# Values projected when they are made: a per-tile product by the value matrix moved into the preparation of the values (layer 0 of a two-layer attention kernel)

## Chip, cores and metric

The kernel runs on one core of one Trainium2 chip. The metric is the device time of one launch in microseconds (us). TensorE is called PE (its weight loads PEld), VectorE DVE, ScalarE ACT, GpSimd POOL and SyncE SP, as in the profile.

## The reference

Input x has 4 batches of 128 channels and 64 x 64 = 4096 tokens. Layer 0 is full attention on group-normalised x with 64-wide queries and keys and 128-wide values; layer 1 is causal attention on layer-normalised tokens, followed by a recurrent network. All data are fp32.

```python
# layer 0; xf = group norm of x, as (b, c, n)
q = einsum('oc,bcn->bon', Wq, xf) + bq
k = einsum('oc,bcn->bon', Wk, xf) + bk
v = einsum('oc,bcn->bon', Wv, xf) + bv
probs = softmax(einsum('bci,bcj->bij', q, k), axis=-1)
x = x + einsum('bcj,bij->bci', v, probs)
# layer 1; t = x as tokens (b, n, c)
t = t + causal_attention(ln(t), Wq1, Wk1, Wv1)
t = t + ffn(ln(t), W, V, gamma, beta)     # batch norm, then y = sigmoid(Wx_t + V y) over the tokens
```

The weights of each value's sum add up to one, so the projection by Wv can be done before or after that sum, and the bias bv is simply added to x.

## The kernel before

X is held with channels on the 128 partitions and tokens along the free axis. Queries are worked on in tiles of 512 tokens (8 tiles a batch), keys in units of 256 tokens. The batches run one after the other, and in each the 8 tiles of layer 0 and then the 8 tiles of layer 1. A layer-0 tile has 16 units; layer 1 is causal, so its tile c has 2(c+1) units. The work of one unit is:

- `score`: products of keys and queries into the PSUM pair `ps` (four fp32r products on L895 in layer 0, four records for two fp32 products on L888 in layer 1), and ACT's exp into the SBUF tile `s` (L897, L901; three `s` buffers);
- `product`: DVE adds `s` to the running `total` (L929; L924 for the first unit), and PE multiplies the values by `s` into the PSUM accumulator `av` (L932, two fp32 products, which the profile shows as four records).

The score of a unit is written ahead of the product of the unit before it. The values of layer 0, `V0`, are kept in the buffer that is later WX of the last batch, so the profile calls them `WX` in the rows of L932; those of layer 1 are called `V`.

The small work between the units is written as generators which a hand-made list (`todo`, and `ends` for the endings of tiles) steps once a unit. The final order on each engine is then set by a scheduler with priorities, which keeps this order nearly everywhere. The generators that matter here:

- `keys0(b, c)` prepares 512 keys and values of layer 0. DVE makes the normalised `xn` (called `xg`, L644; two buffers), POOL adds the bias B0v to X in place (L646), PE makes `pk` = keys and queries (L649), ACT and DVE split the keys into high and low parts (L652 to L661; QR, L654, holds the later queries), PE transposes `xn` in four blocks of 128 tokens (L665), and ACT copies the result into `V0` (L666). The eight calls of batch 0 stand at the start and under its first tile; those of batch b+1 stand within layer 1 of batch b.
- `finish` ends a tile. DVE adds the two halves of `total` (`t`, L765), sums over partitions by two 32x32 transposes, small copies and reductions (L767 to L780), and forms `o` = av / sum, scaled by GUARD (L782). Two steps later PE multiplies `o` by the value matrix into `po` (L788: W0v or W1v), and DVE adds `po` / GUARD to X (L794).
- `prepare1` then makes layer 1's values from the new X: PE transposes (L688), DVE takes statistics (L692 to L694) and normalises (L721), POOL takes the root (L561).
- `query1` makes layer 1's queries: `pq` on PE (L730), `q` on DVE (L732). `ffn` prepares the recurrence input (L741 to L757).

`pk`, `pt`, `po`, `pq` and the like share two PSUM buffers, handed out by `misc`. The recurrence (L1000 to L1021) follows after all batches, and a flag at the end decides whether a general kernel runs again.

Of the kernel before, what the change touches and what calls it, by code (L numbers as in the profile page):

```python
# [23 lines left out]
ALU = mybir.AluOpType  # L27
# [3 lines left out]
P = 128  # L31
QT = 512
# [430 lines left out]
GUARD = 2.0**40  # L463
# [11 lines left out]
def fast_kernel(  # L475
# [9 lines left out]
    nc = tc.nc  # L485
# [14 lines left out]
    X, X2 = {}, {}  # L500
# [14 lines left out]
    def load(src, shape, name):  # L515
        t = const.tile(shape, F32, name=name)
        nc.scalar.dma_start(out=t, in_=src)
        return t
# [8 lines left out]
    W0v = load(w0v, [P, C], "W0v")  # L527
    W1v = load(w1v, [P, C], "W1v")
# [6 lines left out]
    ident = const.tile([P, P], F32, name="ident")  # L535
# [27 lines left out]
    with ExitStack() as actx:  # L563
# [10 lines left out]
        def misc(name):  # L574
            return ps_m.tile([P, QT], F32, tag="m", name=name)

        gn, K0, QR, V0, V1, Q, R1, wt = {}, {}, {}, {}, {}, {}, {}, {}
# [57 lines left out]
        def keys0(b, c):  # L635

            if c == 0:
                K0[b] = kv.tile([P, N], F32R, tag="K0", name=f"K0_{b}")
                QR[b] = kv.tile([P, N // 2], F32, tag="QR", name=f"QR_{b}")
                V0[b] = WX[B - 1].rearrange("p l s -> p (l s)").rearrange("p (n c) -> p n c", c=C)  # L640
            xn = tmp.tile([P, QT], F32, tag="x", name=f"xg_{b}_{c}", bufs=2)
            gmv, grs = gn[b]
            xt = X[b][:, ts(c, QT)]
            nc.vector.tensor_scalar(xn, xt, gmv[:, 0:1], grs, ALU.subtract, ALU.mult)  # L644

            nc.gpsimd.tensor_scalar(xt, xt, B0v, None, ALU.add)  # L646
            yield
            pk = misc(f"pk_{b}_{c}")
            nc.tensor.matmul(pk, lhsT=W0qk.rearrange("p h o -> p (h o)"), rhs=xn, start=True, stop=True)  # L649
            k = tmp.tile([P, QT], F32, tag="k", name=f"k_{b}_{c}")  # L650
            low, up = slice(0, CQ), slice(CQ, P)
            nc.scalar.activation(k[up, :], pk[up, :], AF.Identity, bias=B0qk[up, :])  # L652
            half, col = divmod(c, NQ // 2)
            nc.vector.tensor_scalar(  # L654
                QR[b][ds(half * CQ, CQ), ts(col, QT)], pk[low, :], B0qk[low, :], None, ALU.add
            )
            yield
            high = tmp.tile([P, QT], F32, tag="h", name=f"kh_{b}_{c}", bufs=2)
            nc.vector.tensor_scalar(high[up, :].bitcast(I32), k[up, :].bitcast(I32), HIGH, None, ALU.bitwise_and)
            nc.vector.tensor_tensor(K0[b][up, ts(c, QT)], k[up, :], high[up, :], ALU.subtract)  # L660
            nc.scalar.copy(K0[b][low, ts(c, QT)], high[up, :])  # L661
            yield
            pt = misc(f"pt0_{b}_{c}")
            for j in range(4):
                nc.tensor.transpose(pt[:, ts(j, P)], xn[:, ts(j, P)], ident)  # L665
            nc.scalar.copy(V0[b][:, 4 * c : 4 * c + 4, :], pt.rearrange("p (j c) -> p j c", j=4))  # L666
            yield

        def query0(b, c):
# [90 lines left out]
        def finish(b, layer, c, off, w, av, total):  # L760

            name = f"{layer}_{b}_{c}_{off}"
            k = w // 32
            t = tmp.tile([P, QT], F32, tag="a", name=f"t_{name}")[:, :w]
            nc.vector.tensor_tensor(t, total[:, 0, :w], total[:, 1, :w], ALU.add)  # L765
            tt = tmp.tile([P, QT], F32, tag="b", name=f"tt_{name}")[:, :w]
            nc.vector.transpose(tt, t)  # L767
            part = small.tile([P, 16], F32, tag="part", name=f"part_{name}")
            nc.vector.tensor_reduce(part[:, :k], tt.rearrange("p (k j) -> p k j", j=32), AX.X, ALU.add)
            yield  # L770
            side = small.tile([32, 4, 16], F32, tag="side", name=f"side_{name}")
            for q in range(4):
                nc.vector.tensor_copy(side[:, q, :k], part[ds(32 * q, 32), :k])
            z = small.tile([P, 16], F32, tag="z", name=f"z_{name}")
            nc.vector.tensor_reduce(z[0:32, :k], side[:, :, :k].rearrange("j q k -> j k q"), AX.X, ALU.add)
            nc.vector.reciprocal(z[0:32, :k], z[0:32, :k])
            for q in range(1, 4):
                nc.vector.tensor_copy(z[ds(32 * q, 32), :k], z[0:32, :k])
            rb = tmp.tile([P, 16, 32], F32, tag="a", name=f"rb_{name}")[:, :k, :]
            nc.vector.transpose(rb, z[:, :k].unsqueeze(2).to_broadcast([P, k, 32]))  # L780
            o = tmp.tile([P, QT], F32, tag="b", name=f"o_{name}")[:, :w]
            nc.vector.scalar_tensor_tensor(  # L782
                o, rb.rearrange("p k j -> p (k j)"), GUARD, av[:, :w], ALU.mult, ALU.mult
            )
            yield
            yield
            po = misc(f"po_{name}")[:, :w]
            nc.tensor.matmul(po, lhsT=W1v if layer else W0v, rhs=o, start=True, stop=True)  # L788
            cols = ds(c * QT + off, w)
            xt = X[b][:, cols]  # L790
            if layer and c == 0:
                X2[b] = xpool.tile([P, N], F32, tag="X2", name=f"X2_{b}")
            dst = X2[b][:, cols] if layer else xt
            nc.vector.scalar_tensor_tensor(dst, po, 1.0 / GUARD, xt, ALU.mult, ALU.add)  # L794
            yield


# [35 lines left out]
        def begin_tile(b, layer, c):  # L833

            if layer == 0:
                if c == 0 and b:
                    for k in range(NQ):
                        whole(("k0", b, k))
                    put(("q0", b, 0), query0(b, 0))
                if c == 1 and b == 0:  # L840
                    put(("m1",), merge1())
                if c == 3 and 0 < b < B - 1:
                    for k in range(NQ):
                        whole(("f", b - 1, k, 0))
                    load_x(b + 1)
                if c == (5 if b else 2) and b + 1 < B:
                    put(("gn", b + 1), gn_stats(b + 1))
                if c == NQ - 1:
                    put(("q1", b, 0), after(b, 0))
                whole(("q0", b, c))  # L850
                if c + 1 < NQ:
                    put(("q0", b, c + 1), query0(b, c + 1))
            else:
                if c == 0 and b + 1 < B:
                    whole(("gn", b + 1))
                    for k in range(NQ):
                        put(("k0", b + 1, k), keys0(b + 1, k))
                whole(("q1", b, c))
                if (b, 1, c) in following:
                    d = following[b, 1, c]  # L860
                    todo.insert(0, ("q1", b, d))
                    made["q1", b, d] = after(b, d)
# [47 lines left out]
        def product(i):  # L910
# [30 lines left out]
            if u == n - 1:  # L941
                for key in list(ends):
                    whole(key)
                key = ("e", b, layer, c, off, w)
                made[key] = finish(b, layer, c, off, w, av, total)
                ends.append(key)
# [9 lines left out]
        for k in range(NQ):  # L956
            put(("k0", 0, k), keys0(0, k))
# [12 lines left out]
    with ExitStack() as fctx:  # L970
# [75 lines left out]
        for b in range(B):  # L1046
            for h in range(2):
                cols = ts(h, N // 2)
# [71 lines left out]
```

## Time and profile before

| what | value |
|---|---|
| median of 3 runs | 2593.09 us (2592.93 to 2595.2) |
| the profiled execution | 2594.39 us, its span 2592.4 us |
| mean granted TensorE clock | 0.991 |
| DVE / ACT / POOL busy | 68% / 44% / 8% |
| HBM read / written | 15.14 MB / 14.68 MB |

A row of the profile names line, engine, operation and "out<-in" by the program's tile names without buffer numbers, then the number of records. An fp32 product appears as two matmul records and two weight loads, a transpose as one of each: so L788's 32 products by W0v show as x64, and the 32 x 4 transposes of L665 as x128. The ends of matmul records are modelled, and rows of one engine may overlap. "Idle" after a bar is time in which the engine stood still just before such a row, with what ended it.

### The profile page before, as it was taken

What the parts mean: (1) busy time and instruction counts of PE and PEld (TensorE: products, weight loads), DVE (VectorE), ACT (ScalarE), POOL (GpSimd) and SP (SyncE); (2) the same over time, 40 slices, a digit from 0 to 9 for tenths busy, and PEclk for the clock granted to TensorE, in tenths of its full rate; (3) what the DMA queues carried; (4) which work ended last, traced back from release to release, by engine and by line L of the source; (5) the groups of instructions that cost most, each with busy time, mean ns of one, the idle gap of its engine ahead of it and who ended that gap; (6) DMA issues with size and microseconds to landing.
All of it is one profiled execution on the core that took longest, in us unless ns stands there. A gap on an engine that the chain in (4) does not pass through costs nothing.

```text
span 2592.4 us, 21739 instructions
## 1 busy us (share of the span) xinstructions
PE 2519.8 (97%) x7372; PEld 1345.1 (52%) x7372; DVE 1760.3 (68%) x3513; ACT 1139.7 (44%) x1386; POOL 219.7 (8%) x297
## 2 busy tenths in 40 slices
PE   7999999999999999999999999999999999999975
PEld 4555554444555555444555555444455555544552
DVE  7776667567867667666876666765786766776564
ACT  4444444444444444444444444444444444344444
POOL 2010001101000100010100010110100000000005
PEclk9999999999999999999999999999999999999988
DMA  2000000000100000000100000000010000000013
GB/s 72 1 0 1 0 1 13 9 4 4 37 0 1 0 1 5 13 5 8 37 0 1 1 0 1 13 9 5 5 37 0 1 1 1 0 1 1 0 65 131
DMA packets 11943, 31.28 MB, mean 12 GB/s; under 512 B 2096, under 2 KB 2864, under 8 KB 10032
## 3 DMA queue, kind: packets, MB, share of 16 engines
q1 hardware_dynamic: 8928, 24.12, 2.6%
q10 hardware_dynamic: 2896, 5.71, 0.6%
q8 instruction: 59, 0.97, 0.2%
q14 instruction: 60, 0.49, 0.1%
HBM read 15.14 MB, written 14.68 MB: 12 GB/s over the span
## 4 chain that ended last, share of the span: by engine, by line
PE 89%; DVE 6%; issue 2%; ACT 1%; POOL 1%; DMA 0%; SPq 0%; POOLq 0%; ACTq 0%; DVEq 0%
PE av L932 48%; PE ps L895 17%; PE ps L888 17%; PE po L788 2%; DVE total L929 1%; PE py L1020 1%; PE pq L730 1%; PE pk L649 1%; POOL rstd_f L561 1%; PE pw_f L747 1%; ACT WX L1021 1%; PE pt L688 1%; DVE lst_f L692 0%; PE pt L665 0%; DVE w_f L751 0%
## 5 line engine op out<-in xcount | busy, mean ns | idle before, releaser
L929 DVE TENSOR_TENSOR total<-total,s 128x1024 f32<-128x1024 f32 (+4 forms) x802 | 881.6, 1103 | 553.4 <-ACT s L897 308.9
L932 PE MATMUL av<-s,WX 128*128 128x512 f32 x2048 | 964.4, 593 | 3.4 <-ACT s L897 3.4
L897 ACT ACTIVATE s<-ps,shift 128x1024 f32<-128x1024 f32 x512 | 569.2, 1114 | 772.9 <-PE ps L895 749.0
L895 PE MATMUL ps<-q,K 128*128 128x512 f32 x2048 | 759.7, 493 | 2.1 <-DVE K L660 1.5
L901 ACT ACTIVATE s<-ps,zero,R 128x512 f32<-128x512 f32 (+1 forms) x590 | 399.9, 729 | 458.9 <-PE ps L888 458.3
L932 PEld LDWEIGHTS av<-s,WX 128*128 128x128 f32 x2048 | 382.2, 189 | 312.0 <-issue 270.0
L895 PEld LDWEIGHTS ps<-q,K 128*128 128x128 f32 x2048 | 386.7, 189 | 291.0 <-issue 236.3
L932 PE MATMUL av<-s,V 128*128 128x512 f32 (+3 forms) x1180 | 504.7, 549 | 0.6 <-ACT s L901 0.6
L888 PE MATMUL ps<-q,X 128*128 128x512 f32 (+3 forms) x1180 | 501.9, 548 | 0.0
L888 PEld LDWEIGHTS ps<-q,X 128*128 128x128 f32 x1180 | 222.6, 190 | 239.7 <-issue 228.2
L932 PEld LDWEIGHTS av<-s,V 128*128 128x128 f32 x1180 | 218.8, 191 | 226.1 <-issue 201.6
L561 POOL TENSOR_TENSOR rstd<-rstd,mhalf 128x4 f32<-128x4 f32 x32 | 32.7, 1022 | 1015.5 <-DVE rstd L560 1015.5
L904 POOL TENSOR_SCALAR_AFFINE_SELECT s<-s 128x128 f32<-128x128 f32 x128 | 46.5, 367 | 523.0 <-ACT s L901 522.4
L646 POOL TENSOR_SCALAR X<-X,B0v 128x512 f32<-128x512 f32 x32 | 59.6, 1865 | 243.8 <-DVE xg L644 238.1
L794 DVE SCALAR_TENSOR_TENSOR X<-po,X 128x512 f32<-128x512 f32 (+1 forms) x65 | 44.1, 678 | 51.3 <-PE po L788 50.9
L752 ACT COPY WX<-w_f 128x512 f32<-128x512 f32 (+1 forms) x33 | 35.3, 1069 | 93.1 <-DVE w_f L751 93.1
L561 POOL TENSOR_TENSOR rstd_f<-rstd_f,mhalf 128x4 f32<-128x4 f32 (+1 forms) x33 | 36.1, 1094 | 398.6 <-DVE rstd_f L560 398.6
L721 DVE TENSOR_SCALAR V<-pt,lmv,rstd 128x128 f32<-128x128 f32 x128 | 43.7, 404 | 35.8 <-POOL rstd L561 35.8
L788 PE MATMUL po<-o,W1v 128*128 128x512 f32 (+1 forms) x66 | 34.4, 604 | 16.1 <-DVE o L782 16.1
L679 DVE TENSOR_TENSOR q<-QR,qh 64x512 fp32r<-64x512 f32 x64 | 43.9, 685 | 6.3 <-PE ps L895 5.7
L765 DVE TENSOR_TENSOR t<-total 128x512 f32<-128x512 f32 (+1 forms) x65 | 44.5, 684 | 4.5 <-PE pfw L605 2.5
L782 DVE SCALAR_TENSOR_TENSOR o<-rb,av 128x512 f32<-128x512 f32 (+1 forms) x65 | 43.9, 675 | 4.4 <-DVE rb L780 0.5
(124 smaller groups left out, 1312.5 us busy)
## 6 DMA issues: line engine op xcount, KB each, us to landing
X<-in_x SPq DMA_DIRECT2D x28, 256.0 KB, 5.5
kept<-X SPq DMA_DIRECT2D x24, 256.0 KB, 2.0
Y<-kept SPq DMA_DIRECT2D x6, 1024.0 KB, 7.6
out<-Y SPq DMA_DIRECT2D x3, 1024.0 KB, 9.7
out<-Y ACTq DMA_DIRECT2D x3, 1024.0 KB, 10.2
X<-in_x ACTq DMA_DIRECT2D x4, 256.0 KB, 5.6
out<-X SPq DMA_DIRECT2D x1, 1024.0 KB, 16.1
out<-X ACTq DMA_DIRECT2D x1, 1024.0 KB, 12.6
```

The source lines that it names most:

```text
L561: nc.gpsimd.tensor_tensor(dst, dst, mhalf[:, :n], ALU.pow)
L646: nc.gpsimd.tensor_scalar(xt, xt, B0v, None, ALU.add)
L765: nc.vector.tensor_tensor(t, total[:, 0, :w], total[:, 1, :w], ALU.add)
L788: nc.tensor.matmul(po, lhsT=W1v if layer else W0v, rhs=o, start=True, stop=True)
L794: nc.vector.scalar_tensor_tensor(dst, po, 1.0 / GUARD, xt, ALU.mult, ALU.add)
L888: nc.tensor.matmul(ps[:, h, first[h] : w], lhsT=lhsT, rhs=q[:, off + first[h] : off + w], start=True, stop=True,)
L895: nc.tensor.matmul(ps[:, h, :], lhsT=lhsT, rhs=q[:, k, :], start=k == 0, stop=k == 1)
L897: nc.scalar.activation(s, ps, AF.Exp, bias=shift)
L901: nc.scalar.activation(part, ps[:, h, first[h] : w], AF.Exp, scale=scale, bias=zero)
L904: nc.gpsimd.affine_select(out=edge, in_=edge, pattern=[[1, P]], base=0, channel_multiplier=-1, compare_op=ALU.is_ge, fill=0.0,)
L929: nc.vector.tensor_tensor(t, t, s[:, h, f:w], ALU.add)
L932: nc.tensor.matmul(av[:, first[h] : w], lhsT=V[:, 2 * u + h, :], rhs=s[:, h, first[h] : w], start=u == 0 and h == 0, stop=u == n - 1 and h ...
```

## The change

In `keys0` the four transposes become four products with the same blocks of `xn` as the stationary operand and W0v as the moving one: `V0` then holds the projected values with tokens on the partitions. In `finish`, layer 0 no longer multiplies `o` by W0v: DVE adds `o` / GUARD to X directly in the step that made `o`, and the generator ends two steps earlier. Layer 1's ending is as it was.

```diff
         def keys0(b, c):
...
-            pt = misc(f"pt0_{b}_{c}")
+            pv = misc(f"pv_{b}_{c}")
             for j in range(4):
-                nc.tensor.transpose(pt[:, ts(j, P)], xn[:, ts(j, P)], ident)
-            nc.scalar.copy(V0[b][:, 4 * c : 4 * c + 4, :], pt.rearrange("p (j c) -> p j c", j=4))
+                nc.tensor.matmul(pv[:, ts(j, P)], lhsT=xn[:, ts(j, P)], rhs=W0v, start=True, stop=True)
+            nc.scalar.copy(V0[b][:, 4 * c : 4 * c + 4, :], pv.rearrange("p (j c) -> p j c", j=4))
...
         def finish(b, layer, c, off, w, av, total):
...
-            yield
-            yield
-            po = misc(f"po_{name}")[:, :w]
-            nc.tensor.matmul(po, lhsT=W1v if layer else W0v, rhs=o, start=True, stop=True)
             cols = ds(c * QT + off, w)
             xt = X[b][:, cols]
-            if layer and c == 0:
+            if layer == 0:
+                nc.vector.scalar_tensor_tensor(xt, o, 1.0 / GUARD, xt, ALU.mult, ALU.add)
+                yield
+                return
+            yield
+            yield
+            po = misc(f"po_{name}")[:, :w]
+            nc.tensor.matmul(po, lhsT=W1v, rhs=o, start=True, stop=True)
+            if c == 0:
                 X2[b] = xpool.tile([P, N], F32, tag="X2", name=f"X2_{b}")
-            dst = X2[b][:, cols] if layer else xt
-            nc.vector.scalar_tensor_tensor(dst, po, 1.0 / GUARD, xt, ALU.mult, ALU.add)
+            nc.vector.scalar_tensor_tensor(X2[b][:, cols], po, 1.0 / GUARD, xt, ALU.mult, ALU.add)
             yield
```

In the changed program one line is added above these, so its line numbers are one higher up to the start of `finish` and four higher from its end on (the products by W1v stand on L795, the new addition on L789).

More of the change, by code (lines that the diff above doesn't have):

```diff
@@ L784, in finish @@
             )
+            cols = ds(c * QT + off, w)
+            xt = X[b][:, cols]
+            if layer == 0:
+                nc.vector.scalar_tensor_tensor(xt, o, 1.0 / GUARD, xt, ALU.mult, ALU.add)
+                yield
+                return
             yield
@@ L787, in finish @@
             po = misc(f"po_{name}")[:, :w]
-            nc.tensor.matmul(po, lhsT=W1v if layer else W0v, rhs=o, start=True, stop=True)
-            cols = ds(c * QT + off, w)
-            xt = X[b][:, cols]
-            if layer and c == 0:
+            nc.tensor.matmul(po, lhsT=W1v, rhs=o, start=True, stop=True)
+            if c == 0:
                 X2[b] = xpool.tile([P, N], F32, tag="X2", name=f"X2_{b}")
-            dst = X2[b][:, cols] if layer else xt
-            nc.vector.scalar_tensor_tensor(dst, po, 1.0 / GUARD, xt, ALU.mult, ALU.add)
+            nc.vector.scalar_tensor_tensor(X2[b][:, cols], po, 1.0 / GUARD, xt, ALU.mult, ALU.add)
             yield
```

## The prediction

> **What bounds the kernel now.** I read the page from the top (busy shares, the span in slices, the chain by engine), then the groups of instructions by form, then two stretches of the timeline, then one window sum. From the page:
>
> ```profile
> span 2592.4 us, 21739 instructions
> ...
> PE 2519.8 (97%) x7372; PEld 1345.1 (52%) x7372; DVE 1760.3 (68%) x3513; ACT 1139.7 (44%) x1386; POOL 219.7 (8%) x297
> ...
> PE   7999999999999999999999999999999999999975
> ...
> PE 89%; DVE 6%; issue 2%; ACT 1%; POOL 1%; DMA 0%; SPq 0%; POOLq 0%; ACTq 0%; DVEq 0%
> ```
>
> TensorE (PE) is nine or ten tenths busy in every slice but the first and the last two, and it holds 89% of the chain that ended last. A busy row alone doesn't prove a bound, so I look at the spacing of its instructions. The timeline of PE, columns start, length, what, count:
>
> ```profile
> 78.18 0.38 PE L601 MATMUL pm<-wm 128*128 128x128 f32 x2
> 78.40 1.88 PE L932 MATMUL av<-s,WX 128*128 128x512 f32 x4
> ...
> 148.36 0.60 PE L688 MATMUL pt<-ident,X 128*128 128x128 f32 x4
> 148.80 1.88 PE L932 MATMUL av<-s,WX 128*128 128x512 f32 x4
> ...
> 175.26 1.02 PE L788 MATMUL po<-o,W0v 128*128 128x512 f32 x2
> 176.12 1.88 PE L932 MATMUL av<-s,WX 128*128 128x512 f32 x4
> ```
>
> The lengths overlap; the starts tell what an instruction costs the queue. One fp32 product of 128x512 is two records and moves the next start by 0.86 us (175.26 to 176.12). Four transposes of 128x128 are four records and move it by 0.44 us (148.36 to 148.80), 0.11 each. One fp32 product of 128x128 is two records and moves it by 0.22 us (78.18 to 78.40). These are the three prices of this change. How often the old ones occur, from the groups by form (mean and idle behind the bar):
>
> ```profile
> L788 PE MATMUL po<-o,W0v 128*128 128x512 f32 x64 | 32.7, 593 | 0.8 <-DVE o L782 0.8
> L665 PE MATMUL pt<-ident,xg 128*128 128x128 f32 x128 | 20.3, 282 | 0.0
> ```
>
> The last column matters most: before all 32 products by W0v together PE idled 0.8 us, before the 128 transposes not at all. They stand in a full queue, so what is taken out or put in moves the end, except where PE would have waited anyway.
>
> **What the Trainium skill says.** Perfetto Trace Analysis, section Tensor Engine Instruction: the profiler estimates a matmul's end, it does not observe it. The trace agrees: the rows above say 593 ns for a record whose successor starts 430 ns later; so I use starts. TensorE: Matmul & The Clock Gate, Part 4, gives about 275 ns for a transpose in a kernel; the mean here, 282 ns, agrees as a length, but the spacing of 110 ns decides for throughput. The same page, section LDWEIGHTS, gives columns/1.2 in ns: an estimate of 107 ns for the 128 columns of one weight load. The trace's load rows are longer (146 ns for the transposes, 188 for po by W0v) but are lengths too; the 0.22 us for two records with two loads says that 110 ns suffice. This prices the worst case below. Part 1 of that page says that an idle PE gets half its clock; the trace has that at a stall of 2.1 us before 655.37, after which the four av records at 657.77 last 3.00 us instead of 1.88.
>
> **The change part by part.** There are 4 batches x 8 tiles = 32 layer-0 tiles, each 16 units.
>
> 1. The product at each tile's end goes: 32 x 0.86 = -27.5 us of PE.
> 2. Four transposes become four fp32 products with xn as stationary operand: 4 x (0.22 - 0.11) = 0.44 us more a tile, 32 x 0.44 = +14.1 us. Eight of these tiles are prepared at the start, 24 during layer 1, at the same places of PE's order. Layer 1 of the trace shows PE full there, so nothing hides them. Bounds for a record: 0.107 (the skill's load) to 0.19 us (a whole load row exposed), see the third rival. I take 0.11 since the 128x128 row shows it. The first two tiles run at half clock (their four transposes end 1.06 us after they start, against 0.60 later), so theirs is 0.88 each; the first is on the starting chain, the second lies in the 0.65 us that PE now waits before 21.14 for q, which is as late as the first. Together again 0.9, no correction. W0v's load is issued at 9.00 and lands in 2.0 us, long before 15.8; the DMA queues of SP and ACT keep their order.
> 3. ACT's copy into V0 is the same 128x512 copy (583 ns), 0.44 us later; ACT is 44% busy and waits for PE before most of its exps. DVE's xg of the tile after next reuses the buffer that these products read, so it starts 0.44 us later; in layer 1 DVE prepares it a tile ahead. Nothing.
> 4. X's addition reads o in SBUF instead of po in PSUM: the trace has no such form of it, the nearest rows are this one from PSUM (687 ns) and t from SBUF twice (692 ns). Nothing. It moves directly behind o on DVE, ahead of one to three total additions, where it waited for po before. Seen at 171 us on DVE:
>
> ```profile
> 171.78 0.69 DVE L782 SCALAR_TENSOR_TENSOR o<-rb,av 128x512 f32<-128x512 f32 x1
> 172.39 1.22 DVE L929 TENSOR_TENSOR total<-total,s 128x1024 f32<-128x1024 f32 x1
> 173.96 1.23 DVE L929 TENSOR_TENSOR total<-total,s 128x1024 f32<-128x1024 f32 x1 [0.35 <-ACT s L897]
> 176.32 0.69 DVE L794 SCALAR_TENSOR_TENSOR X<-po,X 128x512 f32<-128x512 f32 x1 [1.14 <-PE po L788]
> ```
>
> DVE's 1.14 us of waiting goes, and it is worth nothing by itself. The two totals behind start up to 0.6 us later; ACT's exp waits for them only through the three s buffers, three units of 2.65 us away.
>
> 5. The next step, layer 1's transposes of X (L688), now stands on PE three units after the tile's end, where po stood, no longer five. Its wait is for X instead of o. Here o ends at 172.47 and po starts at 175.26: 2.8 us of slack, of which the addition takes 0.6. For the tiles up to the seventh of each batch that slack is 1.9 to 3.5 us, apart from the very first tile (0.06 us, and 0.80 us of PE idle). So no new wait, except at the first tile, where X comes 0.6 us after o and the transposes a little later than po: I credit 0.3 us of the 0.8 (bounds 0 and 0.8).
>
> 6. At the start PE waits three times for K on DVE (0.29, 1.00 and 0.20 us idle before 41.98, 49.78 and 70.35). The products put in ahead of these waits may fall into them: credit 0.6 us, bounds 0 and 1.3.
>
> 7. What is late next: the passage from layer 0 to layer 1, where layer 1's tiles are two and four units long and each brings its own ending and query to DVE.
>
> ```profile
> 383.60:405.50 21.90, 21.90 (x61) 10.74 (x59) 21.00 (x62) 8.09 (x13) 3.02 (x8) 1.00 0.00 0
> ```
>
> ```profile
> 404.71 0.74 DVE L654 TENSOR_SCALAR QR<-pk,B0qk 64x512 f32<-64x512 f32 x1
> ...
> 405.51 1.12 PE L730 MATMUL pq<-X,M 128*128 128x512 f32 x2
> ```
>
> The first is a window sum (length, then PE, PEld, DVE, ACT, POOL busy), the second the timeline: DVE is 21.0 of 21.9 us busy, which with the gaps between 62 instructions is full. The pq at 405.51 starts just when DVE has read pk (404.71 + 0.74 = 405.45), whose PSUM buffer it needs; PE waits 0.25 us there already. This stretch loses the po of the eighth tile on PE but nothing on DVE, so PE arrives 0.86 us sooner and waits 0.86 us longer. The three batches with a next batch have this pk: +2.6 us given back, bounds 0 and 2.6. The fourth has no pk and keeps its gain.
>
> Sum: -27.5 + 14.1 - 0.3 - 0.6 + 2.6 = -11.7 us. The profiled execution took 2594.39 us (2592.4 of span and 2.0 around it), 1.3 above the median of 2593.09. So 2582.7 beside the profiled one, and **2581.4 us** as a median.
>
> **Rivals.**
> - The boundary costs nothing, DVE catching up because it no longer idles for po earlier: 2593.1 - 14.3 = 2578.8. For: 1.1 us of DVE idle vanishes at most tiles. Against: DVE starts the dense stretch at the same PE event, with no backlog to save.
> - The tile ends keep PE waiting: DVE takes X late in its order and the transposes find it missing, as at the first tile. It needs over 1.3 us more delay than I see; if it happened by 0.2 us at 28 tiles, +5.6: 2587. Slack measured on o speaks against it.
> - **Slower:** eight weight loads in a row are not hidden under products of only 128 columns. Place: each pv group. A record then costs the whole load, 0.19 us: 8 x 0.19 = 1.52 a tile instead of 0.88, 32 x 0.64 = +20.5, total +8.8: 2601.9. It decides from about 0.155 us a record, where 256 records eat the 11.7. For: such loads come only in twos or threes now, with wider products between. Against: the 0.22 us of L601, and four transposes with a load each at 0.11.
> - The change doesn't do what it says: V0 is read by av alone and both endings write X in place, so one W0v product replaces the other; nothing speaks for it.
>
> **How the numbers follow.** Forecast 0.70, no cost at the boundary 0.15, waits at tile ends 0.09, exposed loads 0.06. The half-clock spell after a stall, 1.7 us, occurs at one of three layer-1 ends now and may come or go with the phase: it and the bounds of steps 5 to 7 widen both sides. Range 2577.0 to 2587.5. A measurement here can tell about 0.2%, 5.2 us, from no change: 2587.9 is the border. Faster 0.90, same 0.04, slower 0.06.
>
> **What would show it.** Right: the L688 rows of layer 0 at po's places without PE idle; pv rows spaced 0.88 us a tile; pq at the boundary with some 1.1 us of waiting for QR; no DVE row X waiting for po in layer 0. Wrong: pv at 1.2 us or more a tile, or idle before L688 at most tiles.

## The result, and the profile after

The changed kernel takes 2579.97 us (median of 5 runs, 2578.95 to 2581.84), against 2593.09 us before (5 runs, 2591.53 to 2596.02): a ratio of 0.9947, 95% interval 0.9936 to 0.9958, or 13.1 us less. The forecast was 2581.4. The profiled execution took 2581.84 us with a span of 2580.0; before, 2594.39 and 2592.4. Between the two profiled executions lie 12.55 us, and 12.4 of span.

The page of the changed kernel, in the parts that were read before:

```profile
span 2580.0 us, 21857 instructions
...
PE 2510.6 (97%) x7436; PEld 1350.5 (52%) x7436; DVE 1761.0 (68%) x3513; ACT 1140.3 (44%) x1386; POOL 227.7 (9%) x297
...
PE   7999999999999999999999999999999999999975
...
PE 88%; DVE 8%; issue 2%; POOL 1%; ACT 1%; POOLq 0%; DVEq 0%; ACTq 0%
```

PE has 64 records more and is busy 9.2 us less; the slices are the same. The count is easily read wrongly: 64 wide records went (0.43 us each by their spacing), 128 transposes went and 256 narrow records came (0.11 each). DVE's share of the chain has grown from 6% to 8%.

The groups by form, with the idle time before them in the last column:

```profile
L666 PE MATMUL pv<-W0v,xg 128*128 128x128 f32 x256 | 35.4, 284 | 0.0
L789 DVE SCALAR_TENSOR_TENSOR X<-o,X 128x512 f32<-128x512 f32 x32 | 22.1, 691 | 0.9
L689 PE MATMUL pt<-ident,X 128*128 128x128 f32 x128 | 19.2, 272 | 0.7 <-DVE X L789 0.7
L731 PE MATMUL pq<-X,M 128*128 128x512 f32 x64 | 33.0, 597 | 2.9 <-DVE QR L655 2.9
```

The new products find no idle PE, so they are paid in full where PE is full. The addition to X lasts 691 ns with `o` in SBUF and 687 with `po` in PSUM. The transposes behind it wait once, for 0.7 us, at the first tile; the other 31 groups find X ready. And `pq` now waits 2.9 us for DVE's read of `pk`, in three places. The timeline has the four places that the forecast named (columns: start, length, engine, line, what, count, and idle before it):

```profile
94.60 0.68 DVE L789 SCALAR_TENSOR_TENSOR X<-o,X 128x512 f32<-128x512 f32 x1
...
95.34 0.66 PE L689 MATMUL pt<-ident,X 128*128 128x128 f32 x4 [0.75 <-DVE X L789]
...
172.50 0.69 DVE L789 SCALAR_TENSOR_TENSOR X<-o,X 128x512 f32<-128x512 f32 x1
...
175.25 0.60 PE L689 MATMUL pt<-ident,X 128*128 128x128 f32 x4
175.68 1.88 PE L936 MATMUL av<-s,WX 128*128 128x512 f32 x4
...
399.37 1.02 PE L795 MATMUL po<-o,W1v 128*128 128x512 f32 x2
...
400.58 0.74 DVE L655 TENSOR_SCALAR QR<-pk,B0qk 64x512 f32<-64x512 f32 x1
...
401.37 1.13 PE L731 MATMUL pq<-X,M 128*128 128x512 f32 x2 [0.97 <-DVE QR L655]
...
481.04 1.05 PE L666 MATMUL pv<-W0v,xg 128*128 128x128 f32 x8
481.93 1.88 PE L936 MATMUL av<-s,V 128*128 128x512 f32 x4
```

At 175.25 the transposes stand where `po` stood at 175.26, and X is ready since 173.19 (172.50 + 0.69), 2.06 us earlier. At 481.04 eight records of the new products move the next start by 0.89 us. At the passage from layer 0 to layer 1, `pq` could start 0.86 us after `po` and starts 2.00 us after it, when DVE has read `pk` (400.58 + 0.74 = 401.32): a loss of 1.14 us, where it was 0.15 before (`po` at 404.50, `pq` at 405.51).

How the gain builds up is best seen at the tiles' ends, the start of DVE's first ending row (`t`, L765 before, L766 after) in both traces:

| end of | before | after | difference |
|---|---|---|---|
| batch 0, layer 0, first tile | 81.34 | 83.19 | +1.85 |
| batch 0, layer 0, eighth tile | 383.67 | 379.41 | -4.27 |
| batch 0, layer 1, eighth tile | 644.50 | 643.44 | -1.06 |
| batch 1, layer 0, eighth tile | 1000.74 | 993.74 | -7.00 |
| batch 1, layer 1, eighth tile | 1261.55 | 1257.78 | -3.77 |
| batch 3, layer 0, eighth tile | 2233.26 | 2222.78 | -10.48 |
| batch 3, layer 1, last whole tile | 2469.32 | 2457.98 | -11.34 |

Layer 0 gains about 0.85 us a tile (batch 1: 7.00 - 1.06 = 5.94 over seven tiles); layer 1, where the next batch's values are made, gives back 3.2 us a batch. Batch 3 prepares nothing and gives nothing back.

### The profile page after: what moved, and what is told of

It reads as the page before. It is cut to its first block, busy times and chain, and to the rows that moved or that the text cites. A ratio compares the mean times of both kernels' runs of the same rounds, so it can differ in the third digit from the quotient of the medians.

```text
span 2580.0 us, 21857 instructions
## 1 busy us (share of the span) xinstructions
PE 2510.6 (97%) x7436; PEld 1350.5 (52%) x7436; DVE 1761.0 (68%) x3513; ACT 1140.3 (44%) x1386; POOL 227.7 (9%) x297
## 4 chain that ended last, share of the span: by engine, by line
PE 88%; DVE 8%; issue 2%; POOL 1%; ACT 1%; POOLq 0%; DVEq 0%; ACTq 0%
PE av L936 47%; PE ps L899 17%; PE ps L892 16%; PE py L1024 2%; DVE total L933 2%; PE po L795 1%; PE pv L666 1%; PE pk L650 1%; PE pq L731 1%; PE pw_f L748 1%; POOL rstd_f L562 1%; PE pt L689 1%; DVE lst_f L693 0%; DVE t L766 0%; ACT s L901 0%
## 5 line engine op out<-in xcount | busy, mean ns | idle before, releaser
L908 POOL TENSOR_SCALAR_AFFINE_SELECT s<-s 128x128 f32<-128x128 f32 x128 | 46.4, 367 | 536.1 <-ACT s L905 535.6
L647 POOL TENSOR_SCALAR X<-X,B0v 128x512 f32<-128x512 f32 x32 | 67.6, 2115 | 251.1 <-DVE xg L645 249.6
L795 PE MATMUL po<-o,W1v 128*128 128x512 f32 (+1 forms) x66 | 34.8, 609 | 16.1 <-DVE o L783 16.1
L766 DVE TENSOR_TENSOR t<-total 128x512 f32<-128x512 f32 (+1 forms) x65 | 44.4, 683 | 4.4 <-PE pfw L606 2.5
L662 ACT CAST K<-kh 64x512 fp32r<-64x512 f32 x32 | 19.7, 617 | 62.3 <-DVE kh L660 62.3
L768 DVE STREAM_TRANSPOSE tt<-t 128x512 f32<-128x512 f32 (+1 forms) x65 | 45.6, 702 | 1.9
```

The costliest lines, as they stand in the source:

```text
L795: nc.tensor.matmul(po, lhsT=W1v, rhs=o, start=True, stop=True)
L908: nc.gpsimd.affine_select(out=edge, in_=edge, pattern=[[1, P]], base=0, channel_multiplier=-1, compare_op=ALU.is_ge, fill=0.0,)
```

## The experiments

The theory: PE's queue sets the time, and the change is the difference of two prices on it, less a wait at the passage. The rivals: one of the prices is other than its row says (hidden work, exposed weight loads); or DVE's earlier addition is what helps. Each kernel was run 5 to 10 times beside runs of the kernel before, whose median was 2593.51 us beside e1 to e4, 2594.73 beside e5 and e6 (on another chip than the others) and 2593.88 beside e7 to e9. The distances to the changed kernel given below are differences of medians from different sessions, so about 1 us in them means little; the ratios are each to the session's own kernel before.

| kernel | median us (range) | ratio to before, 95% interval |
|---|---|---|
| e1, no projection | 2569.83 (2568.86 to 2572.11) | 0.9910, 0.9896 to 0.9923 |
| e2, both projections | 2604.64 (2602.18 to 2604.71) | 1.0038, 1.0025 to 1.0052 |
| e3, products twice | 2606.01 (2605.81 to 2608.42) | 1.0047, 1.0033 to 1.0061 |
| e4, QR on ACT | 2575.76 (2573.91 to 2576.94) | 0.9927, 0.9914 to 0.9941 |
| e5, po later | 2584.94 (2581.82 to 2586.69) | 0.9964, 0.9950 to 0.9977 |
| e6, e4 and e5 | 2580.91 (2578.79 to 2582.62) | 0.9947, 0.9934 to 0.9961 |
| e7, other work held | 2587.90 (2585.81 to 2590.68) | 0.9977, 0.9968 to 0.9986 |
| e8, e4 and e7 | 2586.04 (2582.63 to 2588.46) | 0.9969, 0.9958 to 0.9979 |
| e9, X added later | 2579.91 (2579.48 to 2581.89) | 0.9945, 0.9932 to 0.9959 |

### The two halves apart: e1 and e2

e1 changes the changed kernel, and leaves the projection by W0v out:

```diff
-                nc.tensor.matmul(pv[:, ts(j, P)], lhsT=xn[:, ts(j, P)], rhs=W0v, start=True, stop=True)
+                nc.tensor.transpose(pv[:, ts(j, P)], xn[:, ts(j, P)], ident)
```

> The changed kernel with the four transposes put back in keys0, so that layer 0's values are never projected: only the removal half of the change. If PE's queue sets the time, this takes off the 27.5 us of the 32 products by W0v, gives back about 3 us of longer waiting at the three passages to layer 1, and costs nothing at the values: some 26 us below the kernel before, about 2567. Rival (the removal was partly hidden, and the new products cost less than 0.22 us each): 20 us or less below. Rival (loads exposed, the new products cost about 1 us a tile more than transposes): over 40 us below.

e2 changes the kernel before, and projects layer 0's values twice:

```diff
-                nc.tensor.transpose(pt[:, ts(j, P)], xn[:, ts(j, P)], ident)
+                nc.tensor.matmul(pt[:, ts(j, P)], lhsT=xn[:, ts(j, P)], rhs=W0v, start=True, stop=True)
```

> The kernel before with the four transposes replaced by the four products by W0v, and the product at the tile's end kept, so that layer 0's values are projected twice: only the added half. PE's queue theory: 24 tiles prepared in layer 1 cost 0.45 us each, 10.8, and the eight at the start 1.5 to 3.6 us since PE waits there: 12 to 14.5 us above before, 2605 to 2607.5. The wait of pq for QR stays at 0.25 us, since nothing was taken from the passage. If the loads were exposed: 32 x 1.08 = 34 us above. With e1 the two halves should add up to the change (-13.1).

Measured: the removal alone -23.7 us, the addition alone +11.1 (against their session's 2593.51). Together -12.6, where the change gave -13.1: the halves add up within what the runs scatter. Each is smaller than expected. For the removal, the 26 us do not follow from that text's own terms: 27.5 less 3 is 24.5, and the 0.8 that is missing from this lies within the scatter. The addition falls 0.9 us short of its range, and there the traces show where: the ends of layer 1 in e2 fall back by 3.1 us a batch, not by 8 x 0.44 = 3.5. Two `av` groups a batch, at the diagonal of two tiles in layer 1, waited for POOL's mask (L904, L908 in the changed kernel) in the kernel before, and still do in e1. There the timelines of POOL, PE and PEld read, put together:

```profile
477.09 0.29 POOL L908 TENSOR_SCALAR_AFFINE_SELECT s<-s 128x128 f32<-128x128 f32 x1 [17.42 <-ACT s L905]
477.37 2.08 POOL L647 TENSOR_SCALAR X<-X,B0v 128x512 f32<-128x512 f32 x1
...
478.74 1.93 PE L936 MATMUL av<-s,V 128*128 128x512 f32 x4
...
479.42 1.10 POOL L908 TENSOR_SCALAR_AFFINE_SELECT s<-s 128x128 f32<-128x128 f32 x3
...
479.76 0.30 PEld L936 LDWEIGHTS av<-s,V 128*128 128x128 f32 x2 [0.82 <-POOL s L908]
...
480.51 1.88 PE L892 MATMUL ps<-q,X 128*128 128x512 f32 x4
```

In the changed kernel the same stretch reads:

```profile
482.20 0.29 POOL L908 TENSOR_SCALAR_AFFINE_SELECT s<-s 128x128 f32<-128x128 f32 x1 [16.39 <-ACT s L905]
482.70 0.82 POOL L908 TENSOR_SCALAR_AFFINE_SELECT s<-s 128x128 f32<-128x128 f32 x1 [0.21 <-ACT s L905]
483.51 1.95 POOL L647 TENSOR_SCALAR X<-X,B0v 128x512 f32<-128x512 f32 x1
...
484.30 1.67 PE L936 MATMUL av<-s,V 128*128 128x512 f32 x4
485.80 1.88 PE L892 MATMUL ps<-q,X 128*128 128x512 f32 x4
```

The `av` group takes 1.77 us to the next start in e1 and 1.50 in the changed kernel. The order on POOL differs: in e1 and in the kernel before, POOL's 2 us addition of the bias to X stands between the two masks of the unit, and the `av` waits for the second; in the changed kernel and in e2 both masks stand ahead of it. That is 0.27 us twice a batch in batches 0 to 2, 1.6 us in all. That the longer products made the scheduler choose the other order fits the four traces, but was not tested apart. The wait at the passage goes with the removal, as expected: the product queue's idle time before `pq` for QR is 0 in the kernel before and in e2, 2.9 us in the changed kernel and 3.3 in e1; that of the weight-load queue is 2.5, 2.5, 5.4 and 5.7, in the same order.

### The price of the new products: e3

```diff
             for j in range(4):
                 nc.tensor.matmul(pv[:, ts(j, P)], lhsT=xn[:, ts(j, P)], rhs=W0v, start=True, stop=True)
+            for j in range(4):
+                nc.tensor.matmul(pv[:, ts(j, P)], lhsT=xn[:, ts(j, P)], rhs=W0v, start=True, stop=True)
```

> The changed kernel with the four products of each prepared tile issued twice into the same PSUM buffer (same result). Measures the price alone: at 0.111 us a record 24 x 0.89 = 21.3 us in layer 1 and up to 7.1 (14 at half clock) at the start: 26 to 30 us above the changed kernel, 2606 to 2610. If a run of 16 loads in a row is exposed (0.19 us a record): 24 x 1.52 + 12 = 48 us above.

26.0 us more than the changed kernel, for 256 records: 0.102 us each on the end. By the starts in the traces they cost more, 7.5 us at the start and 7.1 a batch in layer 1, 28.9 in all or 0.113 each; 2.4 us come back because PE's clock, which in the changed kernel's trace fell to half at all three ends of layer 1, did not fall there in e3's. In its timeline the two groups of eight records and what follows:

```profile
491.21 1.05 PE L666 MATMUL pv<-W0v,xg 128*128 128x128 f32 x8
492.10 1.06 PE L668 MATMUL pv<-W0v,xg 128*128 128x128 f32 x8
493.00 1.88 PE L938 MATMUL av<-s,V 128*128 128x512 f32 x4
```

0.89 and 0.90 us: sixteen weight loads in a row, each beside a product of only 128 columns, keep up. The slower rival, 0.19 us a record, is out.

### The wait at the passage: e4

```diff
-            nc.vector.tensor_scalar(
-                QR[b][ds(half * CQ, CQ), ts(col, QT)], pk[low, :], B0qk[low, :], None, ALU.add
-            )
+            nc.scalar.activation(
+                QR[b][ds(half * CQ, CQ), ts(col, QT)], pk[low, :], AF.Identity, bias=B0qk[low, :]
+            )
```

> The changed kernel with the copy QR <- pk moved from DVE to ACT, which frees pk's PSUM buffer earlier at the passage from layer 0 to 1. If pq waits there because DVE is full and reads pk late: the three waits of 0.98 us go, 3 us below the changed kernel, about 2577. Rival (PE only runs into the next DVE result, q for the next tile): less than 1 us. Rival (ACT's exp is held up by 32 more ACT rows of 0.7 us): slower.

4.2 us below the changed kernel, and no run of one reaches into the range of the other. The timeline at the passage:

```profile
396.88 0.68 ACT L653 ACTIVATE k<-pk,B0qk 64x512 f32<-64x512 f32 x1
...
397.58 0.68 ACT L655 ACTIVATE QR<-pk,B0qk 64x512 f32<-64x512 f32 x1
...
399.82 1.02 PE L795 MATMUL po<-o,W1v 128*128 128x512 f32 x2
...
400.41 0.69 DVE L766 TENSOR_TENSOR t<-total 128x512 f32<-128x512 f32 x1
400.68 1.02 PE L731 MATMUL pq<-X,M 128*128 128x512 f32 x2
```

ACT reads `pk` as soon as it has read the keys, at 398.26 both are done, and `pq` starts 0.86 us after `po` without waiting. In the changed kernel the copy stood on DVE behind `t` and ended 1.95 us after the start of `po` (401.32, 399.37); here it ends 1.56 us ahead of it. So the wait was the copy's place in DVE's queue. From the `av` group ahead of the passage to the one behind it there are 6.18 us in the changed kernel (396.15 to 402.33) and 4.93 here (396.60 to 401.53): three times 1.25 is 3.7 of the 4.2 us, and the rest is within the scatter. This version beats both kernels.

### Is the earlier addition to X worth anything: e9

```diff
             if layer == 0:
+                yield
+                yield
                 nc.vector.scalar_tensor_tensor(xt, o, 1.0 / GUARD, xt, ALU.mult, ALU.add)
```

> The changed kernel with the two steps put back ahead of layer 0's addition to X, so that only PE's product is gone and X and the transposes behind it come as late as in the kernel before. If the gain is PE's alone and the early X is worth nothing: within 1 us of the changed kernel, 2579 to 2581. If DVE's earlier addition matters (its 1.1 us of waiting at each of 28 tiles): several us above.

2579.91 us, 0.06 from the changed kernel. But the trace shows that the edit moved less than it was meant to:

```profile
171.33 0.69 DVE L783 SCALAR_TENSOR_TENSOR o<-rb,av 128x512 f32<-128x512 f32 x1
172.06 0.69 DVE L791 SCALAR_TENSOR_TENSOR X<-o,X 128x512 f32<-128x512 f32 x1
```

DVE still adds to X directly behind `o`, at 28 of 32 tiles within 0.4 us, just as in the changed kernel; in the kernel before it did so 2.1 to 4.6 us behind (1.2 at the very first tile). Only PE's transposes of the new X moved, two units later at 24 tiles. So e9 shows that their place is worth nothing, and does not test the earlier X. The traces before and after speak on that: in layer 0 the `av` starts draw apart only in the units whose PE work changed, and by 0.85 us a tile, PE's own price of the product. Nothing is left over for DVE's 1.1 us of waiting or the earlier X.

### The next wait, which did not yield: e5 to e8

The largest waits left in PE's queue, apart from the start, the last tile and the recurrence, are three of 2.1 us at the end of layer 1, which the change didn't touch. The timeline of PE in the changed kernel:

```profile
654.30 1.48 PE L795 MATMUL po<-o,W1v 128*128 128x512 f32 x2 [2.11 <-DVE o L783]
655.58 1.91 PE L748 MATMUL pw_f<-X,FWc 128*128 128x512 f32 x2
657.28 2.42 PE L936 MATMUL av<-s,WX 128*128 128x512 f32 x4
```

The rows behind the wait are longer than elsewhere (1.02 and 1.88): the granted clock was 0.51 from 654.9 to 658.4. e5 puts `po` one unit later:

```diff
             yield
             yield
+            if c == NQ - 1 and b < B - 1:
+                yield
             po = misc(f"po_{name}")[:, :w]
```

> The changed kernel with one more step before layer 1's product po at the last tile of batches 0 to 2, so that it stands one unit (2.65 us) later on PE. It tests what is left in PE's queue where the change touched nothing: 2.1 us of waiting for o, three times, and the half-clock records after it (1.6 us each time in the profiled execution, though not in every one). If both go: 3 x 2.4 + up to 3 x 1.6 = 7 to 12 us below the changed kernel, 2568 to 2573. If only the wait goes and the clock still drops: 6 to 7 below. Rival (PE runs into the next DVE result, lmv for pw_f or K's first tile): under 2 us.

> The changed kernel with both edits, QR on ACT and po one unit later. The two waits lie in different stretches, so the gains should add up: 4.2 us of the first and 7 to 12 of the second, 2564 to 2569. Rival (both draw on the same DVE slack): no more than the better of the two.

e6 has the edits of e4 and e5. e5 came out 5 us above the changed kernel, e6 5 us above e4 (3.3 and 3.9 us when each is measured from its session's kernel before): all the forecasts missed, the rivals' too. The wait for `o` is gone in e5, but further on the timeline shows:

```profile
675.02 0.67 DVE L752 TENSOR_TENSOR w_f<-pw_f,rb_f 128x512 f32<-128x512 f32 x1
...
675.72 1.08 ACT L753 COPY WX<-w_f 128x512 f32<-128x512 f32 x1 [5.33 <-DVE w_f L752]
...
676.61 2.10 ACT L903 ACTIVATE s<-ps,shift 128x1024 f32<-128x1024 f32 x2
...
677.76 3.07 PE L938 MATMUL av<-s,WX 128*128 128x512 f32 x4 [3.23 <-ACT s L903]
```

On ACT the copy of `w_f` stands ahead of two exps. ACT sat idle for 5.3 us until DVE had made `w_f` and started no exp meanwhile; the exp behind the copy, and PE behind that, came 3.2 us late. `po` later makes X later (660.64, where the changed kernel has 656.03), and with it the reload of the batch's buffer and the statistics that DVE takes of it. PE came to this stretch 3.3 us earlier than in the changed kernel, but `w_f` came no earlier (675.02, there 674.46), so all of the gain was lost in the wait. This trace explains only a part of the 5 us, for it is of the fastest of e5's five executions: 2581.82 us at a mean granted clock of 0.991, where the changed kernel took 2578.95 to 2579.97 at 0.991. The other four had 0.989 or 0.990 and took 2583.4 to 2586.7; where their clock fell, no trace shows.

e7 tried the other side, to free DVE for the ending:

```diff
-            for key in list(ends) + todo[:1]:
+            last = any(k[2] == 1 and k[3] == NQ - 1 and k[1] < B - 1 for k in ends)
+            for key in list(ends) + ([] if last else todo[:1]):
```

> The changed kernel where, while the ending of layer 1's last tile (batches 0 to 2) is under way, no other small work is stepped. In e5 moving po later only made ACT's copy into WX and the exp behind it late; here the ending comes earlier on DVE instead, since some 2.5 us of another tile's statistics no longer stand in its chain. If PE's 2.1 us of waiting for o come from that company on DVE: wait and half-clock records go, 6 to 11 us below the changed kernel, 2569 to 2574. Rival (the ending's own chain is long enough): at most 2 us below. Rival as in e5 (the work held back makes ACT late): no gain or up to 4 us above.

> The same, with QR on ACT as in e4 besides. If the two waits are apart, the gain of 4.2 us adds to that of e7: 2565 to 2570. If not, 2576 as e4 alone.

e8 has the edits of e4 and e7. e7 is 8 us above the changed kernel, beyond even its second rival's 4 us, and e8 10 us above e4, so both of its forecasts missed. `po` still waits 2.0 us for `o`, because the edit did not bring `o` forward: in batch 0 DVE put a `total` addition (652.90, 1.18 us) ahead of it, and from the start of `tt` to the end of `o` the ending takes 10.3 us, where it took 9.5. So whether the ending would be quicker on a free DVE was not tested. And the work held back meets the next tile's ending:

```profile
704.58 1.09 ACT L753 COPY WX<-w_f 128x512 f32<-128x512 f32 x1 [4.05 <-DVE w_f L752]
...
705.47 2.10 ACT L901 ACTIVATE s<-ps,shift 128x1024 f32<-128x1024 f32 x2
...
706.62 1.98 PE L936 MATMUL av<-s,WX 128*128 128x512 f32 x4 [1.95 <-ACT s L901]
```

The same chain, `w_f` to ACT's copy to exp to `av`, as in e5. Moving that copy behind the exps, or to another engine, was not tried, so whether the 2.1 us can be had stays open.

## Why the prediction was right

**The two prices (steps 1 and 2).** Read from the starts of records, -0.86 a product and +0.44 a group, they held: -0.85 us a layer-0 tile in the table of tile ends, and 0.89 for the new group where 0.88 was used. The estimate of 107 ns for a weight load from the Trainium skill (TensorE: Matmul & The Clock Gate, section LDWEIGHTS) is not contradicted: in e3 a load and its product together take 0.11 us of the queue, though the load rows there last 196 ns. A load row's length is not what a load costs the queue.

**The starting tiles.** Four transposes at half clock became eight records of 1.91 us. The first group delays the chain and the second falls into the wait for `q`, as argued: `ps` starts at 21.91 instead of 21.14, 0.77 us later, without idle time.

**The X addition and the transposes (steps 4 and 5).** Right in kind: no new wait, and no gain from DVE. The credit of 0.3 us at the first tile was too high: PE idles 0.75 us there instead of 0.80, and by the starts the tile's end gains 0.16 us beside the product. Step 4 had X directly behind `o`; at the first tile of each batch DVE puts a `total` addition between them, and X starts 1.05 us after the end of `o`.

**The waits for K (step 6).** 0.6 credited. Their idle time went from 1.49 to 1.18 us; with the other waits of that stretch 0.5 was hidden, as the six groups put in moved the starts by 2.19 us, not 2.7.

**The passage (step 7).** The wait there before was 0.15 us by the starts, not 0.25. It was forecast to grow by 0.86 us a passage and grew by 0.99 (1.14 - 0.15), 3.0 us in all instead of 2.6. The remaining 0.13 us is DVE's chain from `t` to QR, which takes 21.91 us after and 21.78 before, its rows in another order. e4 shows that this wait is DVE's late read of `pk`.

**What was missing.** The forecast gain was 1.4 us too small in the median. For the profiled executions the whole sum can be laid out by the starts of the same `av` groups in both traces (us, gain negative):

| part | forecast | by the starts |
|---|---|---|
| first two groups, at half clock | +0.88 | +0.77 |
| other six of the start, less the waits for K | +2.04 | +2.19 |
| end of the first tile | -1.16 | -1.03 |
| the other 31 products by W0v | -26.66 | -26.36 |
| three passages | +2.58 | +2.96 |
| 24 groups in layer 1 | +10.56 | +9.26 |
| sum (rounded to -11.7 in the forecast) | -11.76 | -12.21 |
| where PE's clock rose and fell, and what follows | 0 | -0.24 |
| the two spans | | -12.45 |

The one term that was put at nothing is the wait for POOL: it stood in the waits view, 0.27 us looked like nothing, and six of them take 1.6 us off the 24 groups. All other terms together erred by 1.2 us the other way. So the mechanism was right and the closeness is in part luck, two errors that nearly cancel. The clock's part is small here by chance too: 1.1 us gained at the start (the first eight `ps` records last 2.82 us after and 3.75 before), 2.0 lost at the ends of layer 1, 1.1 gained at the end of the kernel. The median's 13.1 us is 0.9 more than the terms give; that is within the interval of the result (0.9936 to 0.9958, or 10.9 to 16.6 us) and is not traced to a place.

## What to carry to other kernels

On an engine that is full, price an edit by the distance between starts of neighbouring records, not by their lengths: here a record of 512 columns cost 0.43 us and one of 128 columns 0.11, each with its weight load, so that one product of 512 columns less and eight records instead of four transposes made half a gain (-0.86 + 0.44). Then look for stretches where the engine is full only because another one is nearly so: there the gain was handed back as a wait, and the lever was the other engine's queue (one 0.7 us row moved from DVE to ACT). Before moving a wait that looks removable, see what stands behind its follow-up work in the queue of every engine. And look in the trace whether an edit moved what it was meant to move: in e9 and e7 the scheduler put the work elsewhere, and the time alone would have been read as an answer.

## What the runs showed that was not expected

- With the longer products, POOL's order came out otherwise: a mask stood ahead of a 2 us addition, and 0.27 us of PE's waiting went, six times.
- Taking 2.1 us of PE idle time out of one place (e5) put 0.9 and 3.2 us into two others, both behind ACT's copy of `w_f`.
- After a wait of 2.1 us at the end of layer 1 PE's clock fell to half for some 3.4 us in one of three cases before and in three of three after. In the seven profiles that keep this order (before, after, e1 to e4, e9) it fell in 11 of 21 cases, at waits of the same length, so the length alone does not decide it.
- Such a fall cost 1.7 us where it came, but in batches 1 and 2 most of it came back. In all 14 of these cases one of two things is seen: the fall, or else a wait some 20 us later, of 1.1 us in the kernel before (`av` at 1295.34, behind the same copy of `w_f` on ACT as in e5), which with its surroundings costs 1.4. So the fall costs 0.3 us net there, and 1.7 only in batch 3, where no such wait follows. A price read at the fall alone, as for e5 and e7, was too high.
